# The skip count taken from a row of the bit tile instead of a second product

## The chip, the cores and the metric

The kernel runs on one core of a Trainium2 chip, as one launch. The metric is the device time of that launch in microseconds (us), the median of three runs. Engine names are those of the profile: PE (matrix products; PEld is its weight loads), DVE (vector), ACT (scalar), POOL, and SP, which issues the transfers.

## The reference

Four layers work on `x` (16 graphs, 1024 nodes, 64 features) with a 0/1 adjacency `adj` (16 x 1024 x 1024). Each computes `x = x + layer(relu(layernorm(x)), adj)`.

Layer 0 is the one that the change touches. It thins the adjacency out (each node with more than 10 neighbours drops every k-th of them, k being half their number, and a link dropped from either side is gone), and then takes, for each node and feature, a weighted sum of three quantiles of the feature over the remaining neighbours:

```
sv = jnp.sort(vals, axis=2)              # the neighbours' values, in order
for tau, wt in zip([0.25, 0.5, 0.75], [0.25, 0.5, 0.25]):
    pos = jnp.clip(tau * (mf - 1.0), 0.0)
    lo, hi = floor(pos), ceil(pos)
    q = gather(lo) * (1.0 - frac) + gather(hi) * frac
    agg = agg + wt * q
```

So six order statistics (`lo` and `hi` of three quantiles) are wanted for each node and feature. A small two-layer network follows. Layer 1 is an average over neighbours, layer 2 an eight-head attention with the adjacency as a bias, layer 3 a product with the adjacency.

## The kernel before

Everything works on 128 partitions and on 512 nodes at a time. Layer 0 is done without a sort per node. Each feature's 1024 values are ranked once (`ranks`, a sorting network on DVE). The sorted values of a feature are cut into 64 buckets of 16; for each node, the counts of neighbours in the buckets and their positions inside a bucket are matrix products of the 0/1 neighbour matrix with weights made from the ranks (`group`, lines 705 to 768). Their results, `cum` (neighbours up to a bucket), and `c0` and `c1` (two halves of a packed word that holds which of a bucket's 16 places are neighbours), cover four pairs of features.

`picks` (line 771) then loops over 16 graphs x 8 groups of 8 features x 2 halves of the nodes x 6 order statistics: 1536 steps. A step runs in three parts, one loop turn apart, so that three steps are under way at a time:

- `compare(n)` (line 805): DVE compares `cum` with the wanted rank (`le`, line 811) and multiplies with `c0` and `c1` (`wa`, line 813, `wb`, line 815), all 128 x 2048. PE sums these into two PSUM tiles (line 832; `prep` starts with a product at line 825): `prep` is the packed word of the bucket that holds the wanted neighbour together with the count of neighbours to be skipped in it, repeated on the 16 partitions of its group, and `val` is the candidate value of each of the 16 places. ACT copies both out: `wi` is `prep` plus 1, with a per-partition bias held in `shifts[:, 5:6]`; `vs` is `val`, scaled by a constant. Both are recorded at line 398, the line of the helper `act`.
- `bits(n)` (line 844): DVE shifts the 32 bits of `wi` left, by an amount of its own for each partition, `to30`, and masks out one bit (`bit`, line 847): each partition has the bit of its place. PE forms the position sum `pz` from two products: `nth` times the upper half of `bit` (line 852) and `plus_k` times the upper half of `wi` (line 853), which adds the skip count.
- `value(n)` (line 856): DVE compares `pz` with 97 and multiplies with `vs` (line 860), so that the value of the one place that matches is left. After every sixth step, PE sums the groups into `agg` (line 866), and DVE and PE weight and add them (lines 875 and 877).

Other work runs beside these steps. `background` does the ranking and the thinning of the next graphs (DVE mostly). `rest` (line 1225) does layers 1 to 3 of the graph whose layer 0 is finished: attention scores `sp` on PE (line 1165), a reduction on DVE (line 1174), the exponential on ACT, transposes `pcols` on PE (line 451) that ACT copies out (`eT`, line 454), and `ao` on PE (line 1184). A counter hands out work of `rest` at .42 units for each loop turn (the last lines of the function). The loop sets only the program order. The order in which instructions stand on each engine is laid down when the program is built: the tile framework's scheduler takes what is ready, by priority, and gives out buffers (`bits` and `wi` share the tag `a2` with 4 buffers; `prep`, `val` and `pz` share the PSUM tag `pa` with 2). `adjoining` (line 400) keeps a group of products together.

Of the kernel before, what the change touches and what calls it, by code (L numbers as in the profile page):

```python
# [8 lines left out]
F32 = mybir.dt.float32  # L9
BF = mybir.dt.bfloat16  # L10
HP = mybir.dt.float16
F8 = mybir.dt.float8e4
I32 = mybir.dt.int32
I16 = mybir.dt.int16
U8 = mybir.dt.uint8
AF = mybir.ActivationFunctionType
OP = mybir.AluOpType
# [4 lines left out]
P = 128  # L22
# [6 lines left out]
KHI = 65536.0  # L29
# [9 lines left out]
def tile_preln_adj_stack(  # L39
# [30 lines left out]
    nc = tc.nc  # L70
# [53 lines left out]
    def sc(name, shape=(P, P), dt=F32):  # L124
        return scrp.tile(list(shape), dt, name=name)
# [3 lines left out]
    identf = const.tile([P, P], F32, name="identf")  # L129
# [87 lines left out]
    nc.vector.tensor_scalar(pblk, prow_i, 4, None, op0=OP.logical_shift_right)  # L217
    nc.vector.tensor_tensor(same, pblk, fblk, OP.is_equal)

    to30 = const.tile([P, 1], I32, name="to30")  # L220
    nc.vector.tensor_scalar(to30, pplr[:, 0:1], 15.0, None, op0=OP.add)


    tri = scr_f[:, 2, :]
    nc.vector.tensor_tensor(tri, pplr, fplr, OP.is_le)
    nc.vector.tensor_tensor(tri, tri, same, OP.mult)
    nc.vector.tensor_scalar(tri, tri, 0.5, None, op0=OP.mult)
    nth = const.tile([P, P], BF, name="nth")
    nc.vector.scalar_tensor_tensor(nth, identf, -32.0, tri, op0=OP.mult, op1=OP.add)

    plus_k = const.tile([P, P], BF, name="plus_k")
    nc.vector.tensor_scalar(plus_k, identf, 1.0 / KHI, None, op0=OP.mult)


    sel_t = const.tile([P, 2, 32], F32, name="sel_t")
# [41 lines left out]
    nc.vector.tensor_scalar(bkt, prow_i[:, 0:1], 1, None, op0=OP.logical_shift_right)  # L277
    nc.vector.tensor_scalar(off[:, 0:1], bkt, 8.0, -SHIFT, op0=OP.mult, op1=OP.add)
    nc.vector.tensor_scalar(off[:, 1:2], bkt, 0.0, None, op0=OP.is_equal)
    shifts = const.tile([P, 6], F32, name="shifts")  # L280
    nc.vector.tensor_scalar(
        shifts[:, 0:1], off[:, 0:1], -1.0, None, op0=OP.mult
    )
# [7 lines left out]
    )  # L291
    nc.vector.tensor_scalar(shifts[:, 3:4], shifts[:, 2:3], FINE, None, op0=OP.mult)
    nc.vector.memset(shifts[:, 4:5], -0.5)
    nc.vector.memset(shifts[:, 5:6], 1.0)

    def at_row(dst, terms):

# [99 lines left out]
    def act(out_, in_, func=AF.Copy, **kw):  # L397
        nc.scalar.activation(out_, in_, func, **kw)  # L398
# [372 lines left out]
    def picks():  # L771

        steps = [
            (b, g, t, q) for b in range(B) for g in range(NG) for t in range(NH) for q in range(NQ)
        ]
        weights, tables, state, vs_of, els = {}, {}, {}, {}, {}  # L780

        def make(el, g, t):
            gen = group(el, g, t, weights)
            tables[el.b, g, t] = next(gen)
            if t == 0 and g < NG - 1:
                todo = [(el, g + 1, 0), (el, g + 1, 1)]
            elif t == 0:
                todo = []
            elif g < NG - 1:
                todo = [(el, g + 1, 2), (el, g + 1, 3)]  # L790
            else:
                todo = [(el.b + 1, 0, pp) for pp in range(4)] if el.b + 1 < B else []
            n = 0
            for _ in gen:
                if n % 2 == 1 and todo:
                    o, g2, pp = todo.pop(0)
                    o = els[o] if isinstance(o, int) else o
                    prepare(o, g2, pp)
                n += 1
                yield None  # L800

        def prepare(el, g, pp):
            weights.setdefault((el.b, g), {})[pp] = pair_weights(8 * g + 2 * pp, el.rk)

        def compare(n):
            b, g, t, q = steps[n]
            el = els[b]
            hs = slice(t * 512, (t + 1) * 512)
            cum, c1, c0 = tables[b, g, t]
            le = a4("le", (P, 4, 512), HP)  # L810
            nc.vector.tensor_tensor(le, cum, bc(el.krow[q][:, None, hs], [P, 4, 512]), OP.is_lt)  # L811
            wa = a4("wa", (P, 4, 512), HP)
            nc.vector.tensor_tensor(wa, le, c0, OP.mult)  # L813
            wb = a4("wb", (P, 4, 512), HP)
            nc.vector.tensor_tensor(wb, le, c1, OP.mult)  # L815
            prep, val = pa("prep"), pa("val")

            rounds = [
                (prep, [sel_w[:, 1, :]] * 4, [wb[:, pp, :] for pp in range(4)]),
                (prep, [sel_w[:, 0, :]] * 4, [wa[:, pp, :] for pp in range(4)]),  # L820
            ] + [
                (val, [el.tab[:, i, 4 * g + pp, :] for pp in range(4)], [le[:, pp, :] for pp in range(4)])
                for i in range(2)
            ]
            nc.tensor.matmul(
                prep, sel_q[:, q, :], el.kq[:, hs], start=True, stop=False, skip_group_check=True
            )

            def made():
                for i, (dst, w, r) in enumerate(rounds):  # L830
                    for pp in range(4):
                        yield nc.tensor.matmul(  # L832
                            dst[32 * pp : 32 * pp + 32, :], w[pp], r[pp], start=i == 2, stop=i in (1, 3),
                            tile_position=(0, 32 * pp), skip_group_check=True,
                        )

            adjoining(made())
            wi = a2("wi")
            act(wi, prep, AF.Identity, bias=shifts[:, 5:6])
            vs = sb.tile([P, 512], F32, tag="v", bufs=8, name="vs")  # L840
            act(vs, val, AF.Copy, scale=1.0 / UP)
            state[n] = [wi, vs]

        def bits(n):
            wi, vs = state[n]
            bit = a2("bit", dt=I32)
            nc.vector.tensor_scalar(  # L847
                bit, wi.bitcast(I32), to30, 0x40000000, op0=OP.logical_shift_left, op1=OP.bitwise_and
            )
            pz = pa("pz")  # L850
            up = lambda x: x.bitcast(BF).rearrange("p (n two) -> p n two", two=2)[:, :, 1]
            nc.tensor.matmul(pz, nth, up(bit), start=True, stop=False)
            nc.tensor.matmul(pz, plus_k, up(wi), start=False, stop=True)  # L853
            state[n] = [pz, vs]

        def value(n):
            b, g, t, q = steps[n]
            el = els[b]
            pz, vs = state.pop(n)
            nc.vector.scalar_tensor_tensor(vs, pz, 97.0, vs, op0=OP.is_equal, op1=OP.mult)  # L860
            vs_of[q] = vs
            if q < NQ - 1:
                return
            agg = pb("agg")
            adjoining(
                nc.tensor.matmul(  # L866
                    agg[32 * (q_ % 4) : 32 * (q_ % 4) + 32, :], sel_t[:, q_ // 4, :], vs_of[q_],
                    start=q_ < 4, stop=q_ > 1, tile_position=(0, 32 * (q_ % 4)),
                    skip_group_check=True,
                )  # L870
                for q_ in range(NQ)
            )
            hs = slice(t * 512, (t + 1) * 512)
            w = a2("w")
            nc.vector.tensor_tensor(w, agg, el.coef[:, hs], OP.mult)
            acc = pb("acc", (8, 512))
            nc.tensor.matmul(acc, sel_c, w, start=True, stop=True)
            nc.scalar.copy(w[:8, :], acc)
            nc.sync.dma_start(el.z[t * D + 8 * g : t * D + 8 * g + 8, t, :], w[:8, :])

        els[0] = arrive(0)
        for r in background(0):
            yield 0.0
        for _ in els[0].stages:
            pass
        for pp in range(4):
            prepare(els[0], 0, pp)
        for _ in make(els[0], 0, 0):
            yield 0.05
        coming = behind = stages = iter(())  # L890


        STEPS = {12: 1, 11: 2, 10: 2, 9: 2, 8: 2, 7: 5, 6: 4, 5: 1, 4: 1, 3: 1, 2: 1, 1: 2}
        last, per = len(steps), NG * NH * NQ
        for n in range(last + 2):
            b, g, t, q = steps[min(n, last - 1)]
            to_go = per - n % per
            if n < last:
                if q == 0 and n + NQ < last:
                    coming = make(els[steps[n + NQ][0]], *steps[n + NQ][1:3])  # L900
                if to_go == per and b + 1 < B:
                    behind = background(b + 1)
                next(coming, None)
                compare(n)
                if to_go == 2 * NQ and b + 1 < B:


                    for _ in behind:
                        pass
                    els[b + 1] = arrive(b + 1)  # L910
                    stages = els[b + 1].stages
                for _ in range(STEPS.get(to_go, 0)):
                    next(stages, None)
            if 0 <= n - 1 < last:
                bits(n - 1)
            next(coming, None)
            if 0 <= n - 2:
                value(n - 2)
                if (n - 1) % per == 0:
                    leave(els.pop(steps[n - 2][0]))  # L920
                    for _ in stages:
                        pass
            next(behind, None)
            yield .42
# [356 lines left out]
```

## Time and profile before

| | before |
|---|---|
| median of 3 runs | 12865.49 us (12863.24 to 12865.96) |
| the profiled execution | 12858.39 us |
| its span, first to last instruction | 12856.6 us |
| PE busy | 11601.9 us, 86209 products |
| DVE busy | 11662.2 us, 21644 instructions |
| ACT busy | 9453.7 us, 16250 instructions |
| mean granted PE clock | 0.986 |

Busy time counts a stretch once, however many instructions of an engine overlap in it. The ends of products are modelled, so PE's busy time is more than the time that its pipeline is taken up. In a row of a group the numbers are: busy time in us, mean nanoseconds of one instruction, and the idle time of the engine just before such instructions with what ended it. The steps of `picks` run from about 364 us to 12465 us after the span's start.

### The profile page before, as it was taken

The page shows a single profiled execution, that of the slowest core. Times are in us where ns is not written, and L with a number is a line of the kernel's source. Part 1 is how long each engine was busy: PE and PEld are TensorE (multiplying, and loading weights), DVE is VectorE, ACT ScalarE, POOL GpSimd, SP SyncE. Part 2 cuts the span into 40 slices and gives each one's busy share as a digit, 9 for nine tenths or more (in the row PEclk, how much of TensorE's full clock was granted, in tenths as well). Part 3 has the DMA queues.
Part 4 walks back from the last instruction along what each step waited for, and adds up shares of the span by engine and source line. Part 5 has one row for each costly group of instructions (what it writes and reads, how often), then busy time and mean ns, then how long its engine had stood idle before and what let it go on. Part 6 is the DMA issues. An engine that isn't in the chain of part 4 may idle for free. (4 is left out here: it accounts for less than half of the span.)

```text
span 12856.6 us, 221392 instructions
## 1 busy us (share of the span) xinstructions
PE 11601.9 (90%) x86209; PEld 5418.0 (42%) x86209; DVE 11662.2 (91%) x21644; ACT 9453.7 (74%) x16250; POOL 24.5 (0%) x138
## 2 busy tenths in 40 slices
PE   0789999999999998999999999999999999999998
PEld 0224444444444444444444444444444444444445
DVE  8999999999998999989899998999989999887873
ACT  0557777777777787777777777777777777787766
POOL 0000000000000000000000000000000000000000
PEclk9999999999999999999999999999999999999999
DMA  3012121221212122121221212122121221212012
GB/s 104 29 40 70 53 90 53 83 66 58 81 53 87 55 64 77 56 87 56 69 67 60 86 54 84 53 62 83 50 87 54 72 73 56 93 31 66 29 61 67
DMA packets 503198, 841.36 MB, mean 65 GB/s; under 512 B 238720, under 2 KB 273664, under 8 KB 502144
## 3 DMA queue, kind: packets, MB, share of 16 engines
q1 hardware_dynamic: 502144, 827.20, 20.7%
q8 instruction: 675, 11.06, 0.4%
q14 instruction: 379, 3.10, 0.1%
HBM read 616.27 MB, written 206.57 MB: 64 GB/s over the span
## 5 line engine op out<-in xcount | busy, mean ns | idle before, releaser
L813 DVE TENSOR_TENSOR wa<-le,c 128x2048 f16<-128x2048 f16 x1536 | 1879.9, 1224 | 161.7 <-PE prep L832 136.4
L727 PE MATMUL px<-valid,cw 128*128 128x512 fp8e4 x8192 | 1979.6, 382 | 0.0
L811 DVE TENSOR_TENSOR le<-cum,krow 128x2048 f16<-128x2048 int16 x1536 | 1878.3, 1223 | 17.3 <-PE val L832 15.2
L815 DVE TENSOR_TENSOR wb<-le,c 128x2048 f16<-128x2048 f16 x1536 | 1878.6, 1223 | 1.2 <-PE prep L832 1.2
L398 ACT ACTIVATE c<-px,shifts 128x512 f16<-128x512 f32 x2048 | 1414.9, 696 | 381.6 <-PE px L748 197.7
L398 ACT ACTIVATE wi<-prep,shifts 128x512 f32<-128x512 f32 x1536 | 1066.6, 694 | 491.2 <-PE prep L832 343.8
L398 ACT ACTIVATE s<-s,nm 128x1024 f32<-128x1024 f32 x1024 | 1167.6, 1142 | 243.7 <-DVE nm L1174 235.9
L727 PEld LDWEIGHTS <-cw 128*128 128x128 f16 x8192 | 801.1, 98 | 1081.1 <-issue 193.4
L1165 PE MATMUL sp<-kT,qT 64*128 64x512 f32 x4096 | 1163.1, 642 | 90.8 <-DVE nm L1174 86.5
L398 ACT ACTIVATE high<-px,shifts 128x512 f16<-128x512 f32 x1024 | 713.8, 697 | 688.1 <-PE px L727 686.8
L451 PE MATMUL pcols<-identf,s 128*128 128x128 f32 x8192 | 1132.8, 281 | 91.6 <-ACT s L398 40.9
L860 DVE SCALAR_TENSOR_TENSOR vs<-pz,vs 128x512 f32<-128x512 f32 x1536 | 1059.5, 690 | 113.6 <-PE pz L853 105.9
L451 PEld LDWEIGHTS pcols<-identf,s 128*128 128x128 f32 x8192 | 889.6, 141 | 597.2 <-ACT eT L454 270.2
L832 PE MATMUL val<-le,tab 128*32 128x512 f16 x12288 | 1112.7, 385 | 20.4 <-DVE vs L860 11.9
L454 ACT COPY eT<-pcols 128x512 f32<-128x512 f32 x2048 | 1105.6, 598 | 17.7 <-PE pcols L451 16.0
L1184 PE MATMUL ao<-eT,v 128*64 128x128 f32 x16384 | 1075.0, 276 | 41.2 <-ACT eT L454 37.9
L398 ACT ACTIVATE vs<-val 128x512 f32<-128x512 f32 x1536 | 926.4, 603 | 185.7 <-PE val L832 108.5
L1184 PEld LDWEIGHTS ao<-eT,v 128*64 128x64 f32 x16384 | 904.3, 137 | 326.5 <-ACT eT L454 249.3
L1174 DVE CUSTOM_DVE_ANT_0 s<-sp,ad,nm 128x512 f32<-128x512 f32 x1024 | 732.5, 751 | 75.7 <-PE sp L1165 75.0
L398 ACT ACTIVATE low<-px,shifts 128x512 f16<-128x512 f32 x1024 | 706.8, 696 | 81.5 <-PE px L739 80.1
L1174 DVE CUSTOM_DVE_ANT_0 s<-sp,ad 128x512 f32<-128x512 f32 x1024 | 686.2, 691 | 85.2 <-PE sp L1165 57.9
L832 PE MATMUL prep<-wb,sel_w 128*32 128x512 f16 x6144 | 639.8, 393 | 134.3 <-DVE wb L815 130.9
(263 smaller groups left out, 19090.6 us busy)
## 6 DMA issues: line engine op xcount, KB each, us to landing
ad<-in_adj_dram SPq DMA_DIRECT2D x768, 512.0 KB
adjT_d<-aT SPq DMA_DIRECT2D x128, 512.0 KB
aT<-adjT_d SPq DMA_DIRECT2D x128, 512.0 KB
md<-sm SPq DMA_DIRECT2D x216, 256.0 KB
sb<-md SPq DMA_DIRECT2D x216, 256.0 KB
rem_d<-rem SPq DMA_DIRECT2D x128, 256.0 KB
left_d<-nb SPq DMA_DIRECT2D x128, 256.0 KB
lr<-left_d SPq DMA_DIRECT2D x256, 128.0 KB
```

Source lines behind the costliest of these rows:

```text
L398: nc.scalar.activation(out_, in_, func, **kw)
L451: nc.tensor.transpose(pt[:, c, :], ad[:, (4 * s + c) * P : (4 * s + c + 1) * P], identf)
L454: nc.scalar.copy(aT[:, 4 * s : 4 * s + 4, :], pt)
L727: yield nc.tensor.matmul(px[pp], w[:, j, :], valid[:, j, :], start=False, stop=j == C - 1, skip_group_check=True,)
L811: nc.vector.tensor_tensor(le, cum, bc(el.krow[q][:, None, hs], [P, 4, 512]), OP.is_lt)
L813: nc.vector.tensor_tensor(wa, le, c0, OP.mult)
L815: nc.vector.tensor_tensor(wb, le, c1, OP.mult)
L832: yield nc.tensor.matmul(dst[32 * pp : 32 * pp + 32, :], w[pp], r[pp], start=i == 2, stop=i in (1, 3), tile_position=(0, 32 * pp), skip_gr ...
L860: nc.vector.scalar_tensor_tensor(vs, pz, 97.0, vs, op0=OP.is_equal, op1=OP.mult)
L1165: nc.tensor.matmul(sps[e], qT[e * D : (e + 1) * D, i * P : (i + 1) * P], kT[e * D : (e + 1) * D, hs], start=True, stop=True,)
L1174: nc.vector.tensor_tensor_reduce(ss[e][:, hs], sps[e], ad[:, hs], -1.0, 3.0e38 if t == 0 else nms[e], op0=OP.add, op1=OP.min, accum_out=nm,)
L1184: nc.tensor.matmul(ao[e * D : (e + 1) * D, :], v[:, j, e * D : (e + 1) * D], eTs[e][:, j, :], start=j == 0, stop=j == C - 1, tile_position ...
```

## The change

`plus_k` and its product go. The skip count reaches `pz` in another way: of the 16 places of a group, the last one (`pplr` equal to 15) needs no sum of earlier places of its own, so its row of the bit tile is used to carry the upper half of `wi`. For that, the shift and the mask become per-partition values: `to30` has two columns, the amount of the shift (0 in a last place) and the mask (bit 30 elsewhere; in a last place the upper half of the word without bit 30). `nth` gets 1/65536 in the rows of the last places and nothing else there. The match value becomes per-partition too (`match`: 97, and 160 in a last place). `wi` is now a plain copy of `prep`, without the 1.

```diff
-    to30 = const.tile([P, 1], I32, name="to30")
-    nc.vector.tensor_scalar(to30, pplr[:, 0:1], 15.0, None, op0=OP.add)
+    to30 = const.tile([P, 2], I32, name="to30")
+    field = sc("field", (P, P))
+    nc.vector.tensor_scalar(field, pplr, 15.0, None, op0=OP.is_equal)
+    keep = sc("keep", (P, P))
+    nc.vector.tensor_scalar(keep, field, -1.0, 1.0, op0=OP.mult, op1=OP.add)
+    nc.vector.tensor_scalar(to30[:, 0:1], pplr[:, 0:1], 15.0, keep[:, 0:1], op0=OP.add, op1=OP.mult)
+    nc.vector.tensor_scalar(
+        to30[:, 1:2], field[:, 0:1], -65536.0 - 1073741824.0, 1073741824.0, op0=OP.mult, op1=OP.add
+    )
+    match = const.tile([P, 1], F32, name="match")
+    nc.vector.tensor_scalar(match, field[:, 0:1], 63.0, 97.0, op0=OP.mult, op1=OP.add)
...
+    nc.vector.scalar_tensor_tensor(tri, identf, -32.0, tri, op0=OP.mult, op1=OP.add)
+    nc.vector.tensor_tensor(tri, tri, keep, OP.mult)
+    nc.vector.tensor_tensor(field, field, same, OP.mult)
     nth = const.tile([P, P], BF, name="nth")
-    nc.vector.scalar_tensor_tensor(nth, identf, -32.0, tri, op0=OP.mult, op1=OP.add)
-
-    plus_k = const.tile([P, P], BF, name="plus_k")
-    nc.vector.tensor_scalar(plus_k, identf, 1.0 / KHI, None, op0=OP.mult)
+    nc.vector.scalar_tensor_tensor(nth, field, 1.0 / KHI, tri, op0=OP.mult, op1=OP.add)
...
             wi = a2("wi")
-            act(wi, prep, AF.Identity, bias=shifts[:, 5:6])
+            nc.scalar.copy(wi, prep)
...
             nc.vector.tensor_scalar(
-                bit, wi.bitcast(I32), to30, 0x40000000, op0=OP.logical_shift_left, op1=OP.bitwise_and
+                bit, wi.bitcast(I32), to30[:, 0:1], to30[:, 1:2], op0=OP.logical_shift_left, op1=OP.bitwise_and
             )
...
-            nc.tensor.matmul(pz, nth, up(bit), start=True, stop=False)
-            nc.tensor.matmul(pz, plus_k, up(wi), start=False, stop=True)
+            nc.tensor.matmul(pz, nth, up(bit), start=True, stop=True)
...
-            nc.vector.scalar_tensor_tensor(vs, pz, 97.0, vs, op0=OP.is_equal, op1=OP.mult)
+            nc.vector.scalar_tensor_tensor(vs, pz, match, vs, op0=OP.is_equal, op1=OP.mult)
```

The sixth column of `shifts`, which held the 1, goes too. The program built from the new kernel has 1536 products and 1536 weight loads fewer on PE, 1536 copies in place of 1536 activations on ACT, and 5 instructions more on DVE, all of them in the setup; the scheduler also puts about a third of DVE's 21,600 instructions at another place among their neighbours.

More of the change, by code (lines that the diff above doesn't have):

```diff
@@ L279, in tile_preln_adj_stack @@
     nc.vector.tensor_scalar(off[:, 1:2], bkt, 0.0, None, op0=OP.is_equal)
-    shifts = const.tile([P, 6], F32, name="shifts")
+    shifts = const.tile([P, 5], F32, name="shifts")
     nc.vector.tensor_scalar(
@@ L293, in tile_preln_adj_stack @@
     nc.vector.memset(shifts[:, 4:5], -0.5)
-    nc.vector.memset(shifts[:, 5:6], 1.0)
     def at_row(dst, terms):
```

## The prediction

> **What bounds the kernel now.** I read the busy times first, then the groups with shapes kept apart, then the steps' stretch cut at every 48th `bit` (32 pieces), then DVE's waits and the chain.
>
> ```profile
> PE 11601.9 (90%) x86209; PEld 5418.0 (42%) x86209; DVE 11662.2 (91%) x21644; ACT 9453.7 (74%) x16250; POOL 24.5 (0%) x138
> ```
>
> Two engines stand side by side at 90%, so neither alone bounds. The chain of waits, which can be followed back as far as 6454 us, agrees: 21% of the span lies on PE, 19% on DVE, 7% on ACT. The pieces tell more (width in us, then PE, PEld, DVE, ACT, POOL busy):
>
> ```profile
> 4824.00:5227.00 403.00, 363.74 (x2719) 169.62 (x2715) 385.08 (x714) 297.04 (x507) 1.43 (x8) 0.98 0.23 72
> 5602.00:5989.00 387.00, 360.36 (x2693) 169.35 (x2691) 370.13 (x740) 295.23 (x507) 1.26 (x8) 1.00 0.25 77
> 6769.00:7144.00 375.00, 351.95 (x2687) 164.98 (x2686) 350.02 (x597) 291.71 (x507) 0.00 (x0) 1.00 0.20 62
> 7530.00:7908.00 378.00, 356.84 (x2697) 165.87 (x2694) 337.28 (x609) 297.98 (x517) 0.00 (x0) 1.00 0.19 56
> 11394.00:11763.00 369.00, 352.72 (x2687) 164.45 (x2686) 297.92 (x496) 296.10 (x517) 0.00 (x0) 1.00 0.13 38
> ```
>
> Each piece is the same 48 steps; PE's and ACT's work hardly differ, DVE's does, with the ranking beside it. In the first two, DVE idles 18 and 17 us, and a piece with 15 us more DVE work is 16 us longer: DVE bounds. In the last three the width stays at 369 to 378 us while DVE's work falls from 350 to 298: PE, with ACT in its loop, bounds. Of the 32 pieces 13 are of the first kind (384 to 412 us each), 6 like the third, 8 like the fourth, 3 like the last; 2 at the start have no later layers beside them.
>
> The groups that the change touches, with those that give prices:
>
> ```profile
> L398 ACT ACTIVATE wi<-prep,shifts 128x512 f32<-128x512 f32 x1536 | 1066.6, 694 | 491.2 <-PE prep L832 343.8 <-PE val L832 67.5 <-issue 63.0
> L454 ACT COPY eT<-pcols 128x512 f32<-128x512 f32 x2048 | 1105.6, 598 | 17.7 <-PE pcols L451 16.0
> L860 DVE SCALAR_TENSOR_TENSOR vs<-pz,vs 128x512 f32<-128x512 f32 x1536 | 1059.5, 690 | 113.6 <-PE pz L853 105.9 <-ACT vs L398 6.0
> L847 DVE TENSOR_SCALAR bit<-wi,to 128x512 int32<-128x512 int32 x1536 | 744.1, 484 | 1.3 <-ACT wi L398 0.7 <-ACT cw L398 0.5
> L853 PE MATMUL pz<-wi,plus_k 128*128 128x512 bf16 x1536 | 599.6, 390 | 0.0
> ```
>
> DVE waits only 105.9 us for `pz`, in 109 of 1536 steps. So a shorter path to `pz` is worth little by itself; what counts is the load on PE.
>
> **What the skill says.** The Trainium skill, "TensorE: Matmul & The Clock Gate", section "Back-to-back issue gap", gives 215.7 ns from start to start for 512 columns, less than one product's duration. The trace agrees: `plus_k`'s row has 390 ns, yet the next product starts 0.22 us after it.
>
> ```profile
> 6018.88 0.40 PE L852 MATMUL pz<-bit,nth 128*128 128x512 bf16 x1
> ...
> 6019.12 0.39 PE L853 MATMUL pz<-wi,plus_k 128*128 128x512 bf16 x1
> ...
> 6019.34 0.38 PE L825 MATMUL prep<-kq,sel_q 128*128 128x512 f16 x1
> ```
>
> "ScalarE: Activation LUTs", section "What ACT_TABLE_LOAD costs", says that each [128,1] operand of an ACTIVATE adds about 93 ns. The trace: 694 ns for `wi` with a bias operand, 603 for `vs` with a constant scale, 91 apart. "VectorE: DVE Perf Modes", section "Scalar operands", says that a scalar may be a constant or a [P, 1] operand and gives no price; the trace has one:
>
> ```profile
> L655 DVE TENSOR_SCALAR nr<-nr x16: 419/421/425, 320.6 to 11790.0; 128x1024 int16<-128x1024 int16 x16
> L654 DVE TENSOR_SCALAR nr<-m,r_tau x16: 476/478/481, 319.8 to 11789.0; 128x1024 int16<-128x1024 int16 x16
> L636 DVE TENSOR_SCALAR n<-m,q_tau,q_add x16: 539/546/560, 319.4 to 11713.1; 128x1024 int16<-128x1024 int16 x16
> L1174 DVE CUSTOM_DVE_ANT_0 s<-sp,ad x1024: 665/690/736, 1110.7 to 12804.6; 128x512 f32<-128x512 f32 x171
> L1174 DVE CUSTOM_DVE_ANT_0 s<-sp,ad,nm x1024: 731/750/798, 1114.0 to 12806.2; 128x512 f32<-128x512 f32 x171
> ```
>
> With none, one and two such operands an equal-sized instruction takes 421, 478 and 546 ns; reading PSUM, one operand takes 690 to 750.
>
> **The change part by part.**
>
> 1. PE: one product per step goes, 1536 x 0.22 = 338 us of pipeline. Its weight load (98 ns) runs under other products: nothing.
> 2. ACT: `wi` from an activation (694) to a copy as in `eT` (598): 96 ns, 1536 x 0.096 = 147 us.
> 3. DVE, `bit`: the mask becomes a second operand, 546 - 478 = 68 ns by L636; 104 us. L847 itself has 484 with one operand, so about 550 is expected. A mask of raw bits might be fetched like a constant: the bounds are 0 and 68; I take 65.
> 4. DVE, `vs`: its first operand, 60 ns by L1174; 92 us. Bounds 0 and 65 (nothing suggests a gain).
> 5. Setup: 5 small DVE instructions more, most of 128x128, so between the 0.17 us of a 128x8 row and the 0.69 us of a 128x512 row each: 1 to 3 us at most. DVE is busy 299 of the 364 us before the steps, so part is hidden; I count nothing, and up to 3 us if that cover is gone.
>
> Per piece of 48 steps: PE -10.6 us, ACT -4.6, DVE +6.0. No transfer moves, no buffer and no wait is added. But what is queued behind `bit` on DVE starts 65 ns later, and PE's L852, which waits 305.5 us in total for `bit` with its weight load, gets it that much later.
>
> How much lands? In the second half's chain, counted piece by piece, 41% of the `plus_k` products (71 us), 14% of the `wi` (63 us), 40% of the `vs` (184 us) and 44% of the `bit` (134 us) lie on it. Taken at first order, over 1536 steps: 1536 x (-0.41x0.22 - 0.14x0.096 + 0.40x0.060 + 0.44x0.065) = -78 us. That flatters: a shortened chain soon meets another one, and a lengthened DVE meets none. So I go by kinds of piece:
>
> - 13 DVE-bound pieces: at worst all of DVE's +6.0 counts; by their chain, DVE pieces near 60% (+3.5) and PE's near 25% (-2.7) about cancel. Middle: +2.5 each, +33.
> - 6 like the third: PE could give 5 us, but DVE's own line (350 + 6 + the 17 us of idle seen where it bounds) is 373 of 375. I take -2.5 each, -15.
> - 8 like the fourth: DVE's line is 337 + 6 + 17 = 360 of 378, far off. Half of PE's saving and some of DVE's delay: -5.3 - 0.7 + 2 = -4 each, -32.
> - 3 at the end: DVE off the chain, two thirds of PE's saving, -7 each, -21. The 2 at the start, mostly DVE: +1.5 each, +3. The last 392 us have no steps: 0.
>
> Sum: 33 - 15 - 32 - 21 + 3 = -32 us, against the profiled execution's 12858.4 (span 12856.6 and 1.8 around it): 12826. The median of the runs lies 7 us higher, so 12833 there.
>
> **The rivals.**
>
> - DVE becomes the bound (ends slower). Place: L847 and L860 in the 13 heavy pieces. DVE's 17 us of idle there is not PE's load but the unavoidable turn-round of single waits (it is 14 to 18 us whatever the load), so faster PE takes nothing off it and +6.0 counts whole: 13 x 6 = 78; the six next pieces +3 each = 18; the light ones give -1.5 x 8 and -5 x 3, the start +5: 78 + 18 - 12 - 15 + 5 = +74, 12939. It decides from the point where the heavy pieces keep more than some 85% of DVE's extra, for then they outweigh all that the light ones give. For: DVE's slope of about 1 there. Against: DVE's largest waits are for PE (136.4 us for `prep`, 105.9 for `pz`).
> - It cancels: DVE's cover in the heavy pieces is half of what I take, +5 each, and the light ones go as forecast: 65 - 15 - 32 - 21 + 3 = 0, 12866.
> - PE's backlog is what counts and the chain's first order lands: -78, 12787. For: PE's 21% of the chain. Against: the DVE line in two thirds of the pieces.
> - The redrawn order alone decides. Pieces of one kind of work differ now by some 5 us (402 to 412), so 32 redrawn pieces give about 5 x 5.7 = 28 us either way. This widens each case, and is no case of its own. That the change does not do what it says is ruled out: the built program has the products gone.
>
> **How the numbers follow.** Forecast 0.36, first-order gain 0.11, cancelling 0.20, DVE bound 0.33. Some 26 us (0.2%) is what a measurement can tell from no change. The forecast with the redraw falls partly below that, the cancelling case partly above: faster 0.44, within 0.20, slower 0.36. Low end 12770: the first-order gain with part of the redraw, and also the forecast with a mask that costs nothing (3 us less in each heavy piece, 2 and 1 in the next kinds: 12833 - 39 - 12 - 8 = 12774). High end 12950: the DVE bound with part of its redraw. About one in ten is left out on either side.
>
> **What would show it.** Right: `bit` at about 549 ns, `vs<-pz,match,vs` at 750, `wi` at 598, no L853; DVE busy near 11850, PE busy lower; heavy pieces 0 to 5 us longer, light ones 3 to 5 us shorter. Wrong: heavy pieces longer by 6 us or more with DVE's idle still 17 (the rival), or `bit` and `vs` unchanged in duration (then faster, near 12770).

## The result, and the profile after

The changed kernel takes 12874.1 us (median of 12 runs, 12859.22 to 12886.69), the one before 12865.85 us (12 runs beside them). The ratio is 1.0006, with a 95% interval of 0.9997 to 1.0015: no change that can be measured. The forecast was 12833 us, 0.25% less than before. Pages and traces show one execution of each kernel.

One correction to what stands above on the change: the mask of a last place is the whole upper half of the word, bit 30 included (-65536 as an integer).

The three groups of the changed kernel whose prices were disputed (line numbers have moved by 7 or 8), from its page:

```profile
L847 ACT COPY wi<-prep 128x512 f32<-128x512 f32 x1536 | 909.3, 592 | 550.9 <-PE prep L840 384.2
L867 DVE SCALAR_TENSOR_TENSOR vs<-pz,match,vs 128x512 f32<-128x512 f32 x1536 | 1145.9, 746 | 94.2 <-PE pz L860 89.5
L855 DVE TENSOR_SCALAR bit<-wi,to 128x512 int32<-128x512 int32 x1536 | 831.8, 542 | 2.1 <-ACT wi L847 1.9
```

`wi` went from 694 to 592 ns, `vs` from 690 to 746, `bit` from 484 to 542: each operand costs DVE 56 to 58 ns an instruction. The product with `plus_k` is gone: in the timeline, the next product starts 0.24 us after the single one.

```profile
6022.20 0.40 PE L860 MATMUL pz<-bit,nth 128*128 128x512 bf16 x1
6022.44 0.38 PE L833 MATMUL prep<-kq,sel_q 128*128 128x512 f16 x1
```

So all parts are there at about the price foreseen. The busy times say the same, in the page's first part:

```profile
span 12866.2 us, 217982 instructions
...
PE 11403.3 (89%) x84673; PEld 5318.7 (41%) x84673; DVE 11820.4 (92%) x21649; ACT 9326.3 (72%) x16250; POOL 24.6 (0%) x138
```

PE is busy 199 us less and ACT 127 us less, DVE 158 us more. Where the time went shows in the pieces of 48 steps, cut as in the prediction (width, then PE, PEld, DVE, ACT and POOL busy; the same five pieces of work as there):

```profile
4865.00:5276.00 411.00, 360.37 (x2682) 169.63 (x2683) 392.51 (x718) 295.66 (x512) 1.21 (x8) 0.97 0.21 71
5654.00:6056.00 402.00, 368.48 (x2705) 172.47 (x2703) 375.26 (x740) 294.18 (x510) 1.25 (x8) 0.97 0.23 74
6827.00:7205.00 378.00, 344.02 (x2624) 161.67 (x2626) 355.70 (x598) 286.92 (x502) 0.00 (x0) 0.99 0.19 61
7591.00:7956.00 365.00, 342.43 (x2648) 159.78 (x2637) 343.49 (x616) 290.12 (x510) 0.00 (x0) 1.00 0.19 58
11418.00:11782.00 364.00, 348.16 (x2654) 162.51 (x2650) 303.83 (x498) 293.91 (x520) 0.00 (x0) 1.00 0.12 39
```

The two pieces where DVE bounds grew from 403 to 411 and from 387 to 402 us, the third from 375 to 378; the fourth shrank from 378 to 365, the last from 369 to 364. The same sum over all 32 pieces, by the prediction's kinds, from the two profiled executions:

| kind of piece | number | forecast, us each | measured, us each | measured, total |
|---|---|---|---|---|
| DVE bounds | 13 | +2.5 | +5.5 | +72 |
| third kind | 6 | -2.5 | +2.0 | +12 |
| fourth kind | 8 | -4 | -8.4 | -67 |
| end | 3 | -7 | -5.3 | -16 |
| start | 2 | +1.5 | +4.3 | +9 |

The total is +10 us, as between the two spans (12856.6 and 12866.2). The loss where DVE bounds and the gain where it doesn't cancel each other.

### The profile page after: what moved, and what is told of

The parts are those of the page before. It is cut to its first block, busy times and chain, and to the rows that moved or that the text cites. A ratio compares the mean times of both kernels' runs of the same rounds, so it can differ in the third digit from the quotient of the medians.

```text
span 12866.2 us, 217982 instructions
## 1 busy us (share of the span) xinstructions
PE 11403.3 (89%) x84673; PEld 5318.7 (41%) x84673; DVE 11820.4 (92%) x21649; ACT 9326.3 (72%) x16250; POOL 24.6 (0%) x138
## 5 line engine op out<-in xcount | busy, mean ns | idle before, releaser
L821 DVE TENSOR_TENSOR wa<-le,c 128x2048 f16<-128x2048 f16 x1536 | 1874.0, 1220 | 145.3 <-PE prep L840 117.5
L847 ACT COPY wi<-prep 128x512 f32<-128x512 f32 x1536 | 909.3, 592 | 550.9 <-PE prep L840 384.2
L867 DVE SCALAR_TENSOR_TENSOR vs<-pz,match,vs 128x512 f32<-128x512 f32 x1536 | 1145.9, 746 | 94.2 <-PE pz L860 89.5
L855 DVE TENSOR_SCALAR bit<-wi,to 128x512 int32<-128x512 int32 x1536 | 831.8, 542 | 2.1 <-ACT wi L847 1.9
L406 ACT ACTIVATE cum<-px,shifts 128x512 int16<-128x512 f32 x1024 | 705.7, 699 | 104.5 <-DVE le L819 104.2
```

The costliest lines, as they stand in the source:

```text
L847: nc.scalar.copy(wi, prep)
L867: nc.vector.scalar_tensor_tensor(vs, pz, match, vs, op0=OP.is_equal, op1=OP.mult)
```

## The experiments

Each ran beside runs of the kernel before on the same chip, whose medians in the three sets were 12862.5, 12864.3 and 12863.1 us; differences are against those. Two theories stood against each other: that the engines bound in different pieces, so that DVE's added operands count whole in some and PE's saving in others; or that the effects are small and even ("linear": the same share of them counts in every piece), and that a redrawn order, the scheduler's new order of the instructions, ate a true gain. "By kinds" stands for the mean change in width of a piece of each kind, between the profiled executions.

**DVE's added operands alone.**

```diff
-    to30 = const.tile([P, 1], I32, name="to30")
+    to30 = const.tile([P, 2], I32, name="to30")
...
+    nc.vector.tensor_scalar(to30[:, 1:2], pplr[:, 0:1], 0.0, 1073741824.0, op0=OP.mult, op1=OP.add)
+    match = const.tile([P, 1], F32, name="match")
+    nc.vector.memset(match, 97.0)
...
-                bit, wi.bitcast(I32), to30, 0x40000000, ...
+                bit, wi.bitcast(I32), to30[:, 0:1], to30[:, 1:2], ...
...
-            nc.vector.scalar_tensor_tensor(vs, pz, 97.0, vs, op0=OP.is_equal, op1=OP.mult)
+            nc.vector.scalar_tensor_tensor(vs, pz, match, vs, op0=OP.is_equal, op1=OP.mult)
```

> The kernel before, with two products and the activation kept, but with the mask of bit and the match value of vs read from [P, 1] columns (filled with the same 97 and bit 30 everywhere): only DVE's added operands. Two-regimes theory: bit 542 ns, vs 746; the 13 pieces where DVE bounds take the whole 48 x 0.118 = 5.7 us each, the 6 middle ones 3 to 5, the 8 light ones under 2: total +90 to +125 us. Linear theory (40% of these instructions lie on the chain everywhere, and a redrawn order ate the gain): +70 to +80, spread evenly, some 2.3 us in every piece, light ones too.

Measured: 12944.95 us, +82 (ratio 1.0064, 1.0051 to 1.0076). Two rows of this kernel:

```profile
L850 DVE TENSOR_SCALAR bit<-wi,to x1536: 491/538/571, 361.5 to 12550.8; 128x512 int32<-128x512 int32 x192
L863 DVE SCALAR_TENSOR_TENSOR vs<-pz,match,vs x1536: 697/742/766, 366.3 to 12552.3; 128x512 f32<-128x512 f32 x192
```

The total is a little under what the two-regimes theory wanted, and close to the linear one's. But it does not lie evenly: by kinds, 4.6 us in each of the 13 pieces, 4.6 in the third kind, -1.1 in the fourth, 0.4 at the end, 3.8 at the start. The distribution is that of the first theory.

**One product alone.**

```diff
-            nc.tensor.matmul(pz, nth, up(bit), start=True, stop=False)
-            nc.tensor.matmul(pz, plus_k, up(wi), start=False, stop=True)
+            nc.tensor.matmul(pz, nth, up(bit), start=True, stop=True)
```

> The kernel before without the product with plus_k; it leaves the skip count out of the position sum. Only PE's saving of 0.22 us a step. Two-regimes theory: nothing to -2 us in the 13 pieces where DVE bounds, -8 to -13 in the 8 light ones, -3 in the middle ones, -5 to -10 in the last three: total -90 to -140. Linear theory: 41% of it everywhere, -4.3 us in every piece, -139 in total.

Measured: 12704.85 us, -158 (0.9875, 0.986 to 0.989), more than either theory gave. By kinds: -2.7 where DVE bounds, -2.2, -8.5, -8.4 at the end, -3.1 at the start. Again most is where DVE doesn't bound. The -2.7 where it does is about what the next run shows there without touching PE (-2.6), so it isn't shown to be PE's saving.

**The copy alone.**

```diff
-            act(wi, prep, AF.Identity, bias=shifts[:, 5:6])
+            nc.scalar.copy(wi, prep)
```

> The kernel before with the copy in place of the activation with a bias; it leaves out the 1 that is added to the packed word. Only ACT's saving of 0.096 us a step. Two-regimes theory: nothing where DVE bounds, up to -2 us in the light pieces, -5 to -25 in total. Linear theory: 14% of it, -21 in total, evenly. A change of more than 40 us either way would speak for the order of the instructions as a cause of its own, since ACT is busy for three quarters only.

Measured: 12844.33 us, -18 (0.9986, 0.9979 to 0.9992). The profiled execution was the slowest of its 21 (12861.21 us), as long as that of the kernel before, and so its pieces don't show where the 18 us lie; they do not follow either theory (-2.6 where DVE bounds, +1.2 in the fourth kind, +3.6 at the end). The redraw below moves as much, so that ACT's saving isn't shown to be worth anything.

**PE's and ACT's part without DVE's.**

```diff
-                bit, wi.bitcast(I32), to30[:, 0:1], to30[:, 1:2], ...
+                bit, wi.bitcast(I32), to30[:, 0:1], 0x40000000, ...
...
-            nc.vector.scalar_tensor_tensor(vs, pz, match, vs, op0=OP.is_equal, op1=OP.mult)
+            nc.vector.scalar_tensor_tensor(vs, pz, 97.0, vs, op0=OP.is_equal, op1=OP.mult)
```

> The changed kernel with the mask of bit and the match value of vs put back to the constants 0x40000000 and 97; it leaves out the carrying of the skip count. PE's and ACT's savings without DVE's added operands. Two-regimes theory: the sum of the one-product and the copy runs, -100 to -150 against the kernel before; the pieces where DVE bounds go back to their width before, the light ones stay as short as in the changed kernel or a little shorter. If the redrawn order ate the gain: it is redrawn here too, and the gain stays under 50 us.

Measured: 12705.9 us, -157 (0.9875, 0.9861 to 0.9888): a little more than the -150 foreseen, and the same as one product alone, so that no saving by the copy shows here either. The pieces where DVE bounds are back near their width before (-1.0), the fourth kind is at -11.2. Four of its pieces, the first four of those shown of the changed kernel:

```profile
4774.00:5180.00 406.00, 360.12 (x2648) 167.10 (x2647) 382.49 (x708) 289.85 (x502) 1.79 (x8) 0.97 0.21 72
5551.00:5939.00 388.00, 354.72 (x2664) 168.02 (x2656) 369.99 (x737) 291.28 (x505) 1.26 (x8) 0.98 0.23 76
6702.00:7074.00 372.00, 341.69 (x2622) 161.02 (x2624) 349.42 (x597) 284.21 (x500) 0.00 (x0) 1.00 0.19 62
7465.00:7831.00 366.00, 341.53 (x2619) 160.80 (x2615) 336.99 (x611) 290.31 (x509) 0.00 (x0) 0.99 0.19 58
```

Beside the changed kernel's lines: with the operands added to this kernel, the first goes from 406 to 411 us, the second from 388 to 402, the third from 372 to 378, the fourth from 366 to 365. Over all pieces 161 us are added. This is the finding: the same two operands cost 82 us on the kernel before and about 165 on this one (8 and 157, from the medians). The same holds the other way round: the lighter PE and the copy are worth 157 us without the operands, and 74 with them (82 to 8). The parts do not add up: 82 - 158 - 18 = -94, and +8 was measured. First the page of the operands-alone run, then that of this one:

```profile
span 12943.1 us, 220351 instructions
...
PE 11524.8 (89%) x85188; PEld 5421.8 (42%) x86209; DVE 11830.9 (91%) x21646; ACT 9462.4 (73%) x16250; POOL 24.3 (0%) x138
```

```profile
span 12703.8 us, 218067 instructions
...
PE 11316.0 (89%) x84669; PEld 5307.3 (42%) x84673; DVE 11638.9 (92%) x21649; ACT 9323.9 (73%) x16250; POOL 24.2 (0%) x138
```

The operands add 169 us to DVE's busy time on the kernel before and 182 on this one (110 and 118 ns a step), so the work that is added explains only 13 us of the difference. The theory of two regimes needs mending too: how much of one engine's added work is covered is not fixed, it shifts with the change itself.

**One of the two operands taken back, twice.** First the match value, in a kernel that still computes what the reference does: a place's own weight and the last places' columns are chosen so that a hit gives the same number in every row.

```diff
-    match = const.tile([P, 1], F32, name="match")
-    nc.vector.tensor_scalar(match, field[:, 0:1], 63.0, 97.0, op0=OP.mult, op1=OP.add)
...
-    nc.vector.scalar_tensor_tensor(tri, identf, -32.0, tri, op0=OP.mult, op1=OP.add)
+    half = sc("half", (P, P))
+    nc.vector.tensor_scalar(half, fplr, 15.0, None, op0=OP.is_equal)
+    nc.vector.tensor_scalar(half, half, -0.5, 1.0, op0=OP.mult, op1=OP.add)
+    nc.vector.scalar_tensor_tensor(tri, identf, -40.5, tri, op0=OP.mult, op1=OP.add)
     nc.vector.tensor_tensor(tri, tri, keep, OP.mult)
+    nc.vector.tensor_tensor(tri, tri, half, OP.mult)
     nc.vector.tensor_tensor(field, field, same, OP.mult)
+    nc.vector.tensor_tensor(field, field, half, OP.mult)
...
-            nc.vector.scalar_tensor_tensor(vs, pz, match, vs, op0=OP.is_equal, op1=OP.mult)
+            nc.vector.scalar_tensor_tensor(vs, pz, 80.0, vs, op0=OP.is_equal, op1=OP.mult)
```

> The changed kernel with one match value for all rows: a place's own weight in nth becomes -40 in place of -31.5, and the column of a last place is halved, so that a hit gives 80 everywhere and vs takes a constant again. It computes the whole reference. Theory that DVE bounds nearly everywhere once PE is lighter: the two added operands cost 168 us between the after-with-constants run and the changed kernel, half of that is saved here: -75 to -95 against the changed kernel, -65 to -85 against the one before (ratio about 0.994), with -3 us in each of the 13 heavy pieces and -1 to -2 in the light ones. Linear theory (40% on the chain): -37 against the changed kernel, -29 against the one before.

Measured: 12785.73 us, -79 (0.9938, 0.9925 to 0.995). This version is faster than both kernels. Its row shows the operand gone:

```profile
L870 DVE SCALAR_TENSOR_TENSOR vs<-pz,vs 128x512 f32<-128x512 f32 x1536 | 1046.0, 681 | 84.3 <-PE pz L863 77.6
```

Second, the other operand, with the match column kept:

```diff
-                bit, wi.bitcast(I32), to30[:, 0:1], to30[:, 1:2], ...
+                bit, wi.bitcast(I32), to30[:, 0:1], 0x40000000, ...
```

> The changed kernel with the constant mask 0x40000000 put back in bit, the match column kept; it leaves out the carrying of the skip count. The other half of the added operands. Theory that DVE bounds nearly everywhere: bit back at 484 ns, -75 to -95 against the changed kernel; with the match80 run the two add up to the 168 us. Linear theory: -44.

Measured: 12803.82 us, -60 (0.9954, 0.9942 to 0.9967). Against the changed kernel, which lies 8 us above the kernel before, the two give -87 and -69; together -155, close to the 165. Both save 5.3 us in each of the 13 pieces, where 3 were foreseen of the first, and next to nothing in the fourth kind (-0.8 and +0.8).

**The order alone**, in the kernel before and in the changed one:

```diff
-            yield .42
+            yield .4201
```

> The kernel before with .4201 in place of .42 for the work of the later layers handed out per turn: the same instructions, a third of them at another place among their neighbours. If the order has a price of its own as large as the part of the sum that is missing, the time moves by 30 us or more either way, and the four light pieces near 6000, 7500, 9100 and 10600 us, which all variants shorten, get 5 to 12 us shorter. If order is noise: within 15 us, with those four pieces as long as before.

Measured: 12840.98 us, -23 (0.998, 0.9972 to 0.9989), between the two cases. The profiled execution was the fastest of its 13 (12825.43 us). Four pieces of the fourth kind, in the kernel before and then in this one:

```profile
5989.00:6365.00 376.00, 356.17 (x2697) 167.12 (x2694) 338.05 (x611) 294.56 (x511) 0.00 (x0) 1.00 0.20 59
7530.00:7908.00 378.00, 356.84 (x2697) 165.87 (x2694) 337.28 (x609) 297.98 (x517) 0.00 (x0) 1.00 0.19 56
9077.00:9457.00 380.00, 364.67 (x2672) 166.54 (x2672) 340.26 (x616) 298.89 (x515) 0.00 (x0) 1.00 0.19 56
10631.00:11011.00 380.00, 364.42 (x2692) 168.44 (x2690) 337.64 (x608) 296.28 (x512) 0.00 (x0) 1.00 0.19 55
```

```profile
5982.00:6355.00 373.00, 350.55 (x2656) 166.81 (x2687) 340.49 (x624) 299.47 (x520) 0.00 (x0) 1.00 0.20 60
7526.00:7897.00 371.00, 351.14 (x2657) 166.10 (x2683) 337.12 (x613) 296.35 (x513) 0.00 (x0) 1.00 0.19 57
9068.00:9442.00 374.00, 351.72 (x2635) 165.57 (x2664) 337.64 (x615) 298.88 (x515) 0.00 (x0) 1.00 0.19 56
10613.00:10986.00 373.00, 352.77 (x2669) 166.42 (x2699) 338.33 (x615) 299.82 (x518) 0.00 (x0) 1.00 0.19 57
```

With the same instructions they are 3 to 7 us shorter. So the order has a price of its own, some 23 us here. These four are 23 us shorter together, where the changed kernel made them 55 us shorter; but the other four of the kind got 12 us longer, so that all eight give -11, against -67 in the changed kernel. How much of that gain is the order is known only that roughly. It bears on the finding too: against this order of the kernel before, the operands alone cost 106 us and not 82.

> The changed kernel with .4201 in place of .42: the same instructions in another order. If its order was an unlucky one that ate a true gain, 30 us or more come back (12840 or less). If the gain went to DVE's added operands: within 15 us of the changed kernel, the heavy pieces still 5 to 6 us longer than in the kernel before.

Measured: 12859.54 us, -5 (0.9995, 0.9987 to 1.0004), some 13 us from the changed kernel; its pieces where DVE bounds are still 5.1 us longer than before. No 30 us come back, so an unlucky order is not where the gain went. Against this order the operands cost 152 us: with the order's price allowed for, it is 82 to 106 us on the kernel before and 152 to 165 on the lighter one, and the gap stays.

**Still less for PE**, on the changed kernel:

```diff
-            nc.tensor.matmul(
-                prep, sel_q[:, q, :], el.kq[:, hs], start=True, stop=False, skip_group_check=True
-            )
...
-                            dst[32 * pp : 32 * pp + 32, :], w[pp], r[pp], start=i == 2, stop=i in (1, 3),
+                            dst[32 * pp : 32 * pp + 32, :], w[pp], r[pp], start=i in (0, 2), stop=i in (1, 3),
```

> The changed kernel with one more product of 128 x 512 per step taken from PE: the one with sel_q that starts prep; it leaves out the part of the packed word that holds the skip count. In every kernel with one position product so far the span is DVE's busy time plus 1035 to 1069 us of idle, in those with two it is plus 1112 to 1203. If DVE bounds by now: the idle stays at 1000 to 1050 and the time falls by no more than 50 us against the changed kernel. If PE still counts as it did in the kernel before (157 us for one product less): -100 to -160, with the idle near 900.

Measured: 12851.53 us, -12 (0.999, 0.9984 to 0.9997) against the kernel before, about 20 us under the changed one. Its page:

```profile
span 12854.6 us, 214941 instructions
...
PE 11145.6 (87%) x83132; PEld 5228.3 (41%) x83137; DVE 11818.1 (92%) x21649; ACT 9329.4 (73%) x16250; POOL 23.3 (0%) x138
```

PE is busy 258 us less than in the changed kernel, and the span is only 12 us shorter: a product less was worth 158 us to the kernel before, and another one, though at another place of the step, is worth 12 to 20 us here.

The granted PE clock must be looked at beside this, for it fell from kernel to kernel: 0.986 before and 0.984 with the operands alone, 0.981 in the constants run and 0.979 in the changed kernel, 0.965 in this last one. An estimate of the full-speed time that PE lost is the span times the fall. It is some 26 us from the kernel before to the operands-alone run, and as much from the constants run to the changed kernel, so the clock doesn't make the difference between 82 and 165. From the changed kernel to the last one it is some 180 us, a large part of what the product freed. Still PE's idle time, the span less PE's busy time, grew from 1463 to 1709 us there, so that PE had time left that was not used.

All runs side by side, from their pages (the executions of the copy alone and of the redrawn kernel before lie 17 us above and 16 us below the medians of their runs):

| kernel | products in `pz` | DVE busy, us | span, us | span less DVE busy |
|---|---|---|---|---|
| before | 2 | 11662.2 | 12856.6 | 1194 |
| redrawn before | 2 | 11656.6 | 12823.7 | 1167 |
| copy alone | 2 | 11656.4 | 12859.4 | 1203 |
| operands alone | 2 | 11830.9 | 12943.1 | 1112 |
| one product alone | 1 | 11641.0 | 12706.2 | 1065 |
| after, constants | 1 | 11638.9 | 12703.8 | 1065 |
| after, mask back | 1 | 11732.1 | 12801.4 | 1069 |
| after, match 80 | 1 | 11729.5 | 12783.9 | 1054 |
| after | 1 | 11820.4 | 12866.2 | 1046 |
| redrawn after | 1 | 11816.7 | 12851.3 | 1035 |
| after, less for PE | 1, and none with `sel_q` | 11818.1 | 12854.6 | 1037 |

With one product, the span is DVE's busy time plus 1035 to 1069 us, whatever else is changed. With two, DVE's idle time is larger, and added DVE work fills part of it (1194 falls to 1112). Taking the product away already takes 129 us out of DVE's idle time (1194 to 1065), and there is little cover left for the operands.

Where the idle time lies shows in the pieces again (means, us; "heavy" are the 13 where DVE bounds):

| kernel | heavy: width | DVE busy | DVE idle | fourth kind: width | DVE busy | DVE idle |
|---|---|---|---|---|---|---|
| before | 394.2 | 377.1 | 17.1 | 376.0 | 340.2 | 35.8 |
| operands alone | 398.9 | 382.5 | 16.3 | 374.9 | 344.5 | 30.4 |
| one product alone | 391.6 | 375.9 | 15.6 | 367.4 | 339.7 | 27.7 |
| after, constants | 393.2 | 376.3 | 17.0 | 364.7 | 338.8 | 26.0 |
| after | 399.8 | 382.4 | 17.4 | 367.6 | 344.4 | 23.2 |
| after, less for PE | 401.4 | 382.3 | 19.1 | 366.7 | 344.9 | 21.8 |

In the heavy pieces DVE idles 16 to 19 us in each of these kernels: a lighter PE takes next to nothing off it, and the operands count almost whole. In the fourth kind the product's removal shortens DVE's idle time from 35.8 to 27.7 us; there the operands were covered before (-1.1) and are covered by half after (+2.9). Of the 73 us by which the operands' price over all pieces grew (88 to 161), 32 lie in the fourth kind, 25 in the heavy pieces, 10 at the start, and 6 in the rest. A redraw alone moved the heavy pieces by 14 us and the fourth kind by 11, so this split is rough.

## Why the prediction was right and wrong

The time lies in the stated range, and the two mechanisms, PE's saving and DVE's operands, are those that act. But the forecast of a gain was wrong; what came is the case "it cancels" (12866 given), to which the prediction gave 0.20. The range holds a gain of 95 us as well as a loss of 85, so to lie in it says little. And that the total is near the middle of it is in part luck: the heavy pieces and the third kind came out 66 us above the forecast and the fourth kind 35 us below it, two misses that offset each other.

- Prices: the product (0.22 us from start to start), the copy (96 ns foreseen, 102 measured) and the operands (65 and 60 foreseen, 58 and 56 measured) were right. The mask of raw bits does cost an operand. The section of the Trainium skill that the prediction names for the product has a formula, N/2.4 + 2.5 ns, that comes to 215.8 ns for 512 columns; the figure 215.7 stands under "Wait — 56ns, not 53.3ns?" on the same page. The same section has some 131 ns for each of a stream of such products; here the trace decides, and no two of them start less than 214 ns apart in the kernel before.
- The step that failed is "13 DVE-bound pieces: ... about cancel. Middle: +2.5 each", and with it the third kind's -2.5. Measured were +5.5 and +2.0. DVE's term, taken between +3.5 and +6.0, was +4.6 for the operands alone; the term that was wrong is PE's -2.7 in the heavy pieces. With the operands in, they are 398.9 us wide with two products and 399.8 with one and the copy: PE's saving is worth nothing there. DVE's idle time in them went from 17.1 to 17.4 us, where the prediction's sign for the rival "DVE becomes the bound" was heavy pieces longer by 6 us with DVE's idle still 17. The shares of the chain were those of the kernel that was profiled. They were applied to both sides of the trade at once, as if each side left the other's share as it was.
- The sum by first order (-78) has the same fault. In one order of counting the saving comes whole (-158 for the product alone, where 41% of 338 us is 139), and DVE's side, 81 us in that sum, comes to 165 on the lighter kernel. In the other order DVE's side comes to 82, as in that sum, and the saving is 74 and not 157. So the prediction's reason against that sum, that a shortened chain soon meets another one, was right, but the forecast by pieces allowed too little for it where DVE is busiest.
- For the fourth kind -4 was too small (-8.4). One product alone gives -8.5 there, so PE's saving lands with 80% of its 10.6 us and not half; some of it may be the order, which moved the eight pieces by -7 to +6 us each.
- The rival "DVE becomes the bound" had the mechanism and the price right for its own pieces (+6 and +3 foreseen, +5.5 and +2.0 measured). It missed the fourth kind (-1.5 foreseen, -8.4 measured). Its reading that DVE's idle in the heavy pieces is 14 to 18 us is too narrow: over the 13 pieces of the kernel before it is 11 to 25, with the mean of 17.1.
- The redraw was foreseen at some 28 us either way; the two measured moves are 23 and about 13 us, both down.

Not settled: why the heavy pieces keep 16 to 19 us of DVE's idle time. Of the 1046 us in the changed kernel, 63 lie before the first step, 740 in the steps and 242 after the last one; the longest waits for PE are 118.5 us for `pp`, 117.5 for `prep`, 109.9 for `sp` and 89.5 for `pz`, but what would shorten them no run shows. Open is also whether the copy is worth anything on the kernel before, and what the lower PE clock costs in time.

## What to carry to other kernels

Where two engines are near 90% each, price an edit on the state that the rest of the change leaves behind: take the relief on one engine first, then ask how much idle time the other has left to cover what is added to it. The shares of a chain are not to be multiplied by both halves of a trade at once: in this kernel the sum of the parts was -94 us, and +8 was measured. And cut the profile into equal pieces of work: their widths, and each engine's idle time in them, show which engine bounds where. Here, folding the match value back into the weights, so that DVE reads a constant again, made the trade pay (0.9938).

## What the runs showed of the hardware

A [P, 1] operand in place of a constant cost a DVE instruction of 512 columns 53 to 65 ns, be it the mask of a shift on integers (mean 484 to 542 ns from the kernel before to the changed one; medians 483 to 538 in the operands-alone run, and 477 to 542 from the constants run to the changed kernel) or the comparison value on a PSUM tile (mean 690 to 746; medians 689 to 742, and 681 to 746). On ACT, a plain copy out of PSUM took 592 ns where the activation with a bias operand took 694. In the profiled executions the granted PE clock went down as products were taken away: 0.984 to 0.987 with two in `pz`, 0.979 to 0.982 with one, 0.965 with that of `sel_q` gone too.
